# Graph attention, layer 1: masks by casting and transposing DMAs, bias additions by accumulating DMAs, values scaled from PSUM

## The chip, the cores and the metric

The kernel runs on one core of one Trainium2 chip. The metric is the device time of an execution in microseconds (us). Engines are named as in the profile: PE (TensorE; PEld its weight loads), DVE (VectorE), ACT (ScalarE), POOL (GpSimd), SP (SyncE, which issues DMAs). Each engine works through its own instructions in a fixed order, and waits at an instruction until what it needs has been signalled.

## The reference

Two layers, each a graph step and a feed-forward step with residuals, over 32 graphs ("batches") of 512 nodes with 256 features; `adj` (32 x 512 x 512, int32) holds 0 or 1, with ones at about 1 place in 32. Layer 0 (a graph convolution and a tropical feed-forward) is untouched by the change. Layer 1, cut to what matters:

```python
def _L1_gnn_ref(nodes_embed, node_adj, W, a_src, a_dst, bias, ln_gamma, ln_beta):   # H = 4 heads, HO = 64
    h = jnp.einsum('bnd,hde->bhne', nodes_embed, W)
    e_src = jnp.einsum('bhne,hte->bhtn', h, a_src)
    e_dst = jnp.einsum('bhne,hte->bhtn', h, a_dst)
    for t in range(n_types):
        mask = (node_adj == t + 1).astype(h.dtype)[:, None]
        weight = weight + mask * (e_src[:, :, t, :, None] + e_dst[:, :, t, None, :])
    weight = jax.nn.leaky_relu(weight, negative_slope=0.01)
    weight = jnp.where(node_adj[:, None] == 0, NEG, weight)
    attention = jax.nn.softmax(weight, axis=-1)
    dst = jnp.einsum('bhij,bhje->bhie', attention, h) + bias[None, :, None, :]
    out = jax.nn.relu(dst) + h
    mu = out.mean(axis=-1, keepdims=True)
    var = out.var(axis=-1, keepdims=True)
    out = (out - mu) / jnp.sqrt(var + EPS) * ln_gamma[None, :, None, :] + ln_beta[None, :, None, :]
    ...

def _L1_ffn_ref(x, W_fx, b_fx, W_x, b_x, W_slice, b_slice, temperature, ..., out_w, out_b):
    ...
    sw = jax.nn.softmax((xm @ W_slice.T + b_slice) / temp, axis=-1)      # nodes to 64 slices, 8 heads
    st = jnp.einsum('bhnc,bhng->bhgc', fx, sw) / (snorm + 1e-05)[..., None]
    ot = _hydra(st, ...)                                                # two-way scan over the slices
    out = jnp.einsum('bhgc,bhng->bhnc', ot, sw).transpose(0, 2, 1, 3).reshape(B, N, D_INNER)
    return out @ out_w.T + out_b

x = x + _L1_gnn_ref(_layernorm(x, axis=-1), adj, ...)
x = x + _L1_ffn_ref(_layernorm(x, axis=-1), ...)
```

## The kernel before

The fast path of layer 1 is `layer1_plain`. It works through the 32 batches in 16 groups of two. Two streams of work are woven together. `attentions()` is a generator that does the graph attention of one batch after the other (`prepare`, `attention`, `norm`), and runs up to a few batches ahead. `mixer(g)` does the feed-forward of group g: `slices` for each of the two batches, `tokens`, `scan`, then `unslice`. The main loop gives the attention stream a credit of `PACE` for each step of the mixer; `PACE` follows from `TURNS` and `STEPS`, the numbers of steps that a batch takes in `attention` and in `prepare`. So the order of the instructions on every engine is set by where the generators yield, and the program's order is kept.

`prepare(b)` gathers the 512 rows of x by four indirect DMAs of POOL (L1154), waits three steps, normalizes x (statistics L1126 on DVE, a power on POOL in L31, the scaling on ACT in L1133), adds the layernorm's beta to x on POOL (L1167, it belongs to the sum that comes later), turns the normalized rows by PE (L1142), and computes h and the two attention terms by PE. For each of four tiles of 128 nodes ACT takes from PSUM three exponentials (`mine`, a column of `hv`, `other`) and a copy of h (`ht`, L1186). Then POOL adds the attention's bias to `ht` and writes `hv` (L1189), and DVE scales `hv` by the exponential (L1202). `mine` goes through a PE transpose and a DRAM row (`ownd`) to four tiles `own`, one for each head, spread over all partitions; SP issues these DMAs.

The mask of a batch is made by `masks(b)`, woven into the first steps of `prepare`: SP loads four int32 tiles of adj; ACT makes a bf16 copy of each and sums it (L1093), and squares it and sums that (L1094), which serves a test of the input; PE turns the copies (L1084) and DVE writes them as uint8 into `mask` (L1085).

`attention(b)` has eight turns. In each of them DVE makes two weights (L1213): the larger of `own` and `other`, times the mask.

```python
nc.vector.scalar_tensor_tensor(e, own[h], other[:, j, h : h + 1], mask[:, j, :], ALU.max, ALU.mult)
```

PE multiplies them with `hv` into `avp` (values, L1249) and `adp` (denominators, L1254); ACT copies these, PE turns them back, and DVE multiplies by the reciprocal of the denominators into `av`. Since the weights of a node add up to one after that, a bias added to the values before is a bias added to the result. `norm(b, av)` does the relu, the sum with h, the layernorm and the sum into x, in three steps which are taken between the turns of the next batch's attention: all turns but `i == 2`, ending at the first `i > 2`. In it, DVE computes sums, POOL a power for the variance (`mu`, L1300), and DVE multiplies by it (L1303).

`slices(b)` normalizes x again, adds the output's bias `outb` to x on POOL (L1328), and computes the slice weights `sw`: PE (`lgp`), ACT (exponential, L1336), DVE (L1337, a sum L1340, a product L1342), then PE (`yTp`, L1347). `unslice` multiplies back (L1567), DVE adds to x (L1569), SP stores.

At the end, `over` and `flags` say whether the input kept within what the fast path takes for granted (adj of 0 and 1, each node with an edge, terms of moderate size); if not, a general path runs afterwards. With this input it doesn't run.

Buffers: two each of `mask`, `hv`, `ht`; five of x; one of `av`; four PSUM banks of the kind "any".

## Time and profile before

| what | value |
|---|---|
| median of 3 runs | 4460.33 us (4456.45 to 4473.15) |
| the profiled execution's own time | 4459.08 us |
| its span in the trace | 4456.4 us |
| mean granted TensorE clock | 0.948 |
| busy, PE / DVE / ACT / POOL | 3922.0 / 3347.2 / 2291.6 / 1718.8 us |
| `att` L1213, 512 times on DVE | 392.9 us |
| L1189, L1167, L1328, 32 times each on POOL | 80.2, 77.6, 75.8 us |
| L1085, 128 times on DVE | 85.9 us |

Busy times are sums over the span; the sum over engines is more than the span, since they work beside each other. "Idle before" in a row of groups is the time in which the engine stood still just ahead of such instructions, and the name behind it is what ended that. The chain of waits follows the work that ended last back to the beginning, and so shows which time could shorten the whole. Layer 0 takes the span's first 2380 us or so, layer 1 the rest.

### The profile page before, as it was taken

The page shows a single profiled execution, that of the slowest core. Times are in us where ns is not written, and L with a number is a line of the kernel's source. Part 1 is how long each engine was busy: PE and PEld are TensorE (multiplying, and loading weights), DVE is VectorE, ACT ScalarE, POOL GpSimd, SP SyncE. Part 2 cuts the span into 40 slices and gives each one's busy share as a digit, 9 for nine tenths or more (in the row PEclk, how much of TensorE's full clock was granted, in tenths as well). Part 3 has the DMA queues.
Part 4 walks back from the last instruction along what each step waited for, and adds up shares of the span by engine and source line. Part 5 has one row for each costly group of instructions (what it writes and reads, how often), then busy time and mean ns, then how long its engine had stood idle before and what let it go on. Part 6 is the DMA issues. An engine that isn't in the chain of part 4 may idle for free.

```text
span 4456.4 us, 57911 instructions
## 1 busy us (share of the span) xinstructions
PE 3922.0 (88%) x20311; PEld 2470.6 (55%) x20311; DVE 3347.2 (75%) x7008; ACT 2291.6 (51%) x4756; POOL 1718.8 (39%) x2036
## 2 busy tenths in 40 slices
PE   5568898899988999888997899999999999999987
PEld 4454565566656656545554455555555555555555
DVE  6668887897788987877766777767677877778763
ACT  3345565566564665556654544544545444454433
POOL 2357644664446644454314232332222232332220
PEclk8679999999999999989998999999999999999998
DMA  5546543664436543564422111111111111111100
GB/s 133 160 144 223 190 130 122 210 200 139 156 117 213 187 147 129 162 201 167 138 81 67 36 53 57 56 48 58 51 43 42 53 55 55 58 48 58 41 15 16
DMA packets 235107, 474.21 MB, mean 106 GB/s; under 512 B 38299, under 2 KB 114075, under 8 KB 234804
## 3 DMA queue, kind: packets, MB, share of 16 engines
q0 software_dynamic: 98688, 315.94, 22.2%
q1 hardware_dynamic: 136116, 154.46, 11.0%
q8 instruction: 162, 2.65, 0.2%
q14 instruction: 141, 1.16, 0.1%
HBM read 413.16 MB, written 57.16 MB: 106 GB/s over the span
## 4 chain that ended last, share of the span: by engine, by line
DVE 34%; PE 32%; DMA 11%; issue 9%; POOL 9%; ACT 5%; SPq 0%; POOLq 0%; DVEq 0%; ACTq 0%
DVE att L1213 5%; DVE acc L637 4%; PE clsp L623 3%; PE avp L1249 3%; PE po L652 3%; PE gatep L623 3%; DMA rows<-table,xs 2%; PE yTp L1347 2%; DVE sw L1337 2%; DVE sw L1342 2%; DVE best L598 2%; DMA rows<-table,tops 2%; DVE sst L1340 2%; DMA best<-table,xs 2%; PE xp L1400 1%
## 5 line engine op out<-in xcount | busy, mean ns | idle before, releaser
L623 PE MATMUL clsp<-xnT,wc 128*128 128x512 f32 x1024 | 520.8, 627 | 49.7 <-ACT cls L625 37.6
L623 PE MATMUL gatep<-xnT,wg 128*128 128x512 f32 x1024 | 499.8, 607 | 10.5 <-ACT gate L625 7.7
L652 PE MATMUL po<-wd,acc 128*128 128x256 f32 x2048 | 455.4, 381 | 6.1 <-DVE acc L641 3.8
L1213 DVE SCALAR_TENSOR_TENSOR att<-own,other,mask 128x512 f32<-128x512 f32 x512 | 392.9, 796 | 79.0 <-DMA own<-ownd 79.0
L652 PEld LDWEIGHTS po<-wd,acc 128*128 128x128 f32 x2048 | 388.3, 191 | 72.1 <-issue 9.2
L598 DVE SCALAR_TENSOR_TENSOR best<-rows,xs,best 128x1024 f32<-128x1024 f32 x212 | 274.4, 1295 | 121.9 <-ACT best L592 76.4
L637 DVE SCALAR_TENSOR_TENSOR acc<-past,fld,acc 128x512 f32<-128x512 f32 x448 | 345.7, 775 | 24.9 <-ACT past L636 16.9
L632 ACT ACTIVATE acc<-tz,fld 128x512 f32<-128x512 f32 x256 | 198.8, 777 | 269.3 <-PE tz L630 240.1
L623 PEld LDWEIGHTS gatep<-xnT,wg 128*128 128x128 f32 x1024 | 196.0, 196 | 252.3 <-issue 197.9
L636 ACT ACTIVATE past<-tz,fld 128x512 f32<-128x512 f32 x448 | 291.4, 693 | 68.1 <-DVE acc L637 66.6
L1347 PE MATMUL yTp<-sw,x 128*128 128x512 f32 x512 | 264.6, 655 | 64.3 <-DVE sw L1342 59.6
L595 POOL DMA_INDIRECT rows<-table,xs x212 | 249.5, 1177 | 171.6 <-DVE best L598 119.0
L1249 PE MATMUL avp<-att,hv 128*32 128x512 f32 x2048 | 298.9, 607 | 5.6 <-DVE att L1213 5.6
L623 PEld LDWEIGHTS clsp<-xnT,wc 128*128 128x128 f32 x1024 | 181.5, 198 | 188.1 <-issue 111.8
L434 PE MATMUL pm<-h,adj 128*128 128x258 f32 (+1 forms) x1024 | 181.2, 324 | 99.9 <-DVE keep L427 33.7
L1300 POOL TENSOR_TENSOR mu<-mu,eps 128x16 f32<-128x16 f32 x32 | 111.6, 3487 | 391.1 <-DVE mu L1299 391.0
L1335 PE MATMUL lgp<-wsl,x4T 128*128 128x512 f32 x512 | 242.8, 613 | 15.7 <-ACT sw L1336 6.8
L1154 POOL DMA_INDIRECT x<-x2s,ranks x128 | 135.9, 1062 | 298.1 <-DVE att L1213 148.1
L625 ACT ACTIVATE gate<-gatep,fld 128x512 f32<-128x512 f32 x256 | 175.5, 685 | 142.6 <-PE gatep L623 123.8
L553 POOL DMA_INDIRECT xs<-rows_of,order x128 | 156.1, 1219 | 221.5 <-DVE acc L637 100.8
L1567 PE MATMUL outp<-v,swT 128*128 128x256 f32 x1024 | 227.6, 381 | 0.0
L625 ACT ACTIVATE cls<-clsp,fld 128x512 f32<-128x512 f32 x256 | 176.1, 688 | 93.9 <-PE clsp L623 55.6
(599 smaller groups left out, 8978.1 us busy)
## 6 DMA issues: line engine op xcount, KB each, us to landing
adj<-in_adj POOLq DMA_DIRECT2D x128, 256.0 KB
ai<-in_adj SPq DMA_DIRECT2D x128, 256.0 KB
own<-ownd SPq DMA_DIRECT2D x128, 256.0 KB
rows_of<-keep SPq DMA_DIRECT2D x32, 550.0 KB
x<-in_x SPq DMA_DIRECT2D x32, 512.0 KB
x2s<-xs SPq DMA_DIRECT2D x32, 512.0 KB
out<-x SPq DMA_DIRECT2D x32, 512.0 KB
rows<-table,xs POOLq DMA_INDIRECT x212
```

Of the source, the lines that this page charges most:

```text
L595: nc.gpsimd.indirect_dma_start(out=row, out_offset=None, in_=table, in_offset=bass.IndirectOffsetOnAxis(ap=idxs[:, k : k + 1].bitcast(U32) ...
L598: nc.vector.scalar_tensor_tensor(m, row, vals[:, k : k + 1], m, ALU.add, ALU.max)
L623: nc.tensor.matmul(pf, wf[:, c, f * P : (f + 1) * P], xnT[:, c, :], start=c == 0, stop=c == DC - 1)
L625: nc.scalar.activation(o, pf, fn, bias=fld[:, f, bf : bf + 1], scale=1.0 if fn == AF.Gelu else 0.5)
L636: nc.scalar.activation(r, z, AF.Relu, bias=fld[:, f, AT + b : AT + b + 1])
L637: nc.vector.scalar_tensor_tensor(y, r, fld[:, f, CH + b : CH + b + 1], y, ALU.mult, ALU.add)
L652: nc.tensor.matmul(po[:, i, :], acc[f][:, t * P : (t + 1) * P], wd[:, f, :], start=f == 0, stop=f == FC - 1)
L1213: nc.vector.scalar_tensor_tensor(e, own[h], other[:, j, h : h + 1], mask[:, j, :], ALU.max, ALU.mult)
L1249: nc.tensor.matmul(pv[p][k * HW : (k + 1) * HW, :], hv[:, j, h, e : e + HW], weighed[b, h, j], **ends)
L1335: nc.tensor.matmul(pf, xnT[:, c, t * P : (t + 1) * P], wsl[:, c, :], start=c == 0, stop=c == DC - 1)
L1347: nc.tensor.matmul(py, xn[:, t, c * P : (c + 1) * P], sw[:, t, :], start=t == 0, stop=t == NT - 1)
L1567: nc.tensor.matmul(po[:, :D], swT[:, k, t * P : (t + 1) * P], v[:, k, :], start=k == 0, stop=k == KC - 1)
```

## The change

The masks are made by DMAs: two batches ahead POOL issues a DMA that casts adj (int32) to bf16 into a DRAM tile `short`, and SP issues a transposing DMA from it into `mask`, now bf16. In place of the sums for the test, ACT takes a Square of mask - 0.5 over the whole mask with its sum (each element gives 0.25 if it is 0 or 1), and DVE marks denominators that are not above 0.

The three additions of POOL (beta, the attention's bias, outb) become accumulating DMAs which POOL issues, from rows in a small DRAM table `added`. The attention's bias is added to `av` after the attention, ahead of `norm`, whose three steps start one turn later. `hv` is now written by DVE directly from PSUM, right after the exponential that it is scaled by, for each tile of 128 nodes.

`STEPS` goes from 15 to 11, and with it `PACE` from 0.887 to 0.765. The constants `identb`, `abias`, `beta` and `outb` are gone. In the changed kernel lines have other numbers; those spoken of are L1282 (norm's first instruction on DVE, which takes the relu and adds h), L1292 (the power, L1300 before) and L1295 (the product with it, L1303 before).

```diff
@@ -887,7 +887,7 @@
     HE = HO + 1
     AP = AH // 2
     TURNS = AP * NT + 6
-    STEPS = 15
+    STEPS = 11
     WANTED = 68
     AHEAD = 3
     ATT = 2 * (AHEAD + 2) + AP + 1
@@ -915,8 +915,6 @@
 
         ones = ctile("ones", [P, P])
         nc.gpsimd.memset(ones, 1.0)
-        identb = cst.tile([P, P], BF16, tag="identb", name="identb")
-        nc.vector.tensor_copy(identb, ident)
 
         wa = ctile("wa", [P, DC, AH * HO + 2 * AH])
         for c in range(DC):
@@ -940,14 +938,24 @@
                                  start=c == 0, stop=c == DC - 1)
             nc.vector.tensor_scalar(over[:, : 2 * AH], pn[:, : 2 * AH], SMALL, None, ALU.is_gt)
         yield
-        edges = ctile("edges", [P, 2, B * NT])
-        abias = const("abias", [P, AH * HO], w["gnn_bias"].rearrange("h e -> (h e)").partition_broadcast(P))
+        edges = ctile("edges", [P, B + B * NT])
+        centre = ctile("centre", [P, 1])
+        nc.gpsimd.memset(centre, -0.5)
+        added = dr.tile([3, NT, D], F32, tag="added", name="added", bufs=1)
+        for i, row in enumerate((w["gnn_bias"].rearrange("h e -> (h e)"), w["ln_beta"].rearrange("h e -> (h e)"),
+                                 w["out_b"])):
+            nc.sync.dma_start(added[i], row.partition_broadcast(NT))
+        added = added.rearrange("i t d -> i (t d)")
+        ABIAS, BETA, OUTB = range(3)
+
+        def add_rows(dst, i):
+
+            nc.gpsimd.dma_start(dst, added[i].partition_broadcast(P), accum_op=ALU.add)
+
         gamma = const("gamma", [P, AH * HO], w["ln_gamma"].rearrange("h e -> (h e)").partition_broadcast(P))
-        beta = const("beta", [P, AH * HO], w["ln_beta"].rearrange("h e -> (h e)").partition_broadcast(P))
         bfx = const("bfx", [P, KC, 1], w["b_fx"].rearrange("(k p o) -> p k o", p=P, o=1))
         bfx_eps = ctile("bfx_eps", [P, KC])
         nc.vector.tensor_scalar_mul(bfx_eps, bfx[:, :, 0], -1e-5)
-        outb = const("outb", [P, D], w["out_b"].partition_broadcast(P))
         conv_w = const("conv_w", [P, KC, KW], w["hy_conv_w"][:DI].rearrange("(c p) k -> p c k", p=P))
         conv_b = const("conv_b", [P, KC], w["hy_conv_b"][:DI].rearrange("(c p) -> p c", p=P))
         bc_w = const("bc_w", [S, 2, KW], w["hy_conv_w"][DI:].rearrange("(c p) k -> p c k", p=S))
@@ -1068,44 +1076,24 @@
             nc.scalar.activation(ebsl, ebsl, AF.Exp)
 
         se = ctx.enter_context(tc.tile_pool(name="e1", bufs=2, side="right", reuse_waits="tile"))
-        masked = {}
-
-        def masks(b, bank="any"):
-
-            a, raw = [], []
-
-            def load(t):
-                raw.append(se.tile([P, N], I32, tag="ai", name=f"ai{b}_{t}", bufs=2))
-                nc.sync.dma_start(raw[t], adj[b, t * P : (t + 1) * P, :])
-
-            def turn(t):
-                pt = ps.tile([P, NT, P], BF16, tag=bank, name=f"maskp{b}_{t}")
-                for j in range(NT):
-                    nc.tensor.transpose(pt[:, j, :], a[t][:, j * P : (j + 1) * P], identb)
-                nc.vector.tensor_copy(mask[:, :, t * P : (t + 1) * P], pt)
-
-            load(0)
-            load(1)
-            yield
-            for t in range(NT):
-                n = b * NT + t
-                a.append(se.tile([P, N], BF16, tag="a", name=f"a{b}_{t}", bufs=3))
-                nc.scalar.activation(a[t], raw[t], AF.Identity, accum_out=edges[:, 0, n : n + 1])
-                nc.scalar.activation(raw[t], raw[t], AF.Square, accum_out=edges[:, 1, n : n + 1])
-                if t + 2 < NT:
-                    load(t + 2)
-                if t == 1:
-                    mask = se.tile([P, NT, N], mybir.dt.uint8, tag="mask", name=f"mask{b}")
-                    yield
-                if t > 1:
-                    turn(t - 2)
-                    yield
-            for t in range(NT - 2, NT):
-                turn(t)
-                yield
-            masked[b] = mask
-
-        yield from masks(0, "mm")
+        short, masked = {}, {}
+
+        def shorten(b):
+
+            if b < B:
+                short[b] = dr.tile([N, N], BF16, tag="short", name=f"short{b}", bufs=3)
+                tc.keep_in_program_order(nc.gpsimd.dma_start(short[b], adj[b], max_dma_last_dim=8192))
+
+        def turn(b):
+
+            if b < B:
+                masked[b] = se.tile([P, NT, N], BF16, tag="mask", name=f"mask{b}")
+                nc.sync.dma_start_transpose(masked[b], short.pop(b))
+
+        for b in range(2):
+            shorten(b)
+            yield
+        turn(0)
         yield True
         ps = ctx.enter_context(tc.tile_pool(name="p1", bufs=4, space=PSUM, reuse_waits="tile"))
         sb = ctx.enter_context(tc.tile_pool(name="s1", bufs=2, reuse_waits="tile"))
@@ -1158,20 +1146,23 @@
 
             hv = sb.tile([P, NT, AH, HE], F32, tag="hv", name=f"hv{b}")
             xn = hv.rearrange("p t h e -> p (t h e)")[:, : NT * D].rearrange("p (t d) -> p t d", t=NT)
-            edged = masks(b) if b not in masked else range(3)
-            for i, _ in enumerate(edged):
-                if i < 3 or b not in masked:
-                    yield
-                if i == 2:
-                    normed(xt, xn, f"c{b}")
-                    nc.gpsimd.tensor_add(xt, xt, beta.unsqueeze(1).to_broadcast([P, NT, D]))
-                    yield
+            if b:
+                turn(b)
+            shorten(b + 2)
+            yield
+            yield
+            yield
+            normed(xt, xn, f"c{b}")
+            add_rows(xt.rearrange("p t d -> p (t d)"), BETA)
+            yield
             mask = masked.pop(b)
             xnT = yield from turned(xn, "x3T", f"x3T{b}")
             yield
 
 
             ht = sb.tile([P, NT, AH * HO], F32, tag="ht", name=f"ht{b}")
+            nc.scalar.activation(ht.rearrange("p t e -> p (t e)").bitcast(BF16), mask.rearrange("p t n -> p (t n)"),
+                                 AF.Square, bias=centre, accum_out=edges[:, b : b + 1])
             other = sb.tile([P, NT, AH], F32, tag="other", name=f"other{b}")
             mine = sb.tile([P, AH, NT], F32, tag="mine", name=f"mine{b}")
             for t in range(NT):
@@ -1180,15 +1171,14 @@
                     nc.tensor.matmul(ph[:, : AH * (HO + 2)], xnT[:, c, t * P : (t + 1) * P], wa[:, c, :],
                                      start=c == 0, stop=c == DC - 1)
                 d = ph[:, AH * HO : AH * HO + AH]
+                nc.scalar.activation(hv[:, t, :, HO], d, AF.Exp)
+                nc.vector.tensor_mul(hv[:, t, :, :HO], ph[:, : AH * HO].rearrange("p (h e) -> p h e", h=AH),
+                                     hv[:, t, :, HO:].to_broadcast([P, AH, HO]))
                 nc.scalar.activation(mine[:, :, t], ph[:, AH * (HO + 1) : AH * (HO + 2)], AF.Exp, scale=1.0 - SLOPE)
-                nc.scalar.activation(hv[:, t, :, HO], d, AF.Exp)
                 nc.scalar.activation(other[:, t, :], d, AF.Exp, scale=SLOPE - 1.0)
                 nc.scalar.copy(ht[:, t, :], ph[:, : AH * HO])
                 yield
 
-            nc.gpsimd.tensor_add(hv[:, :, :, :HO], ht.rearrange("p t (h e) -> p t h e", h=AH),
-                                 abias.rearrange("p (h e) -> p h e", h=AH).unsqueeze(1).to_broadcast([P, NT, AH, HO]))
-            yield
             pt = psum("any", f"minep{b}")
             nc.tensor.transpose(pt[: AH * NT, :P], mine.rearrange("p h t -> p (h t)"), ident)
             row = sb.tile([AH * NT, P], F32, tag="turned", name=f"turned{b}", bufs=1)
@@ -1198,8 +1188,6 @@
             own = [wide("own", f"own{b}_{h}", AH + 1) for h in range(AH)]
             for h in range(AH):
                 nc.sync.dma_start(own[h], own_row[h].partition_broadcast(P))
-            for t in range(NT):
-                nc.vector.tensor_mul(hv[:, t, :, :HO], hv[:, t, :, :HO], hv[:, t, :, HO:].to_broadcast([P, AH, HO]))
             ready[b] = mask, ht, hv, other, own
             yield
 
@@ -1254,10 +1242,10 @@
                         nc.tensor.matmul(pd[h * HW : (h + 1) * HW, :], hv[:, j, h, HO:].to_broadcast([P, HW]),
                                          weighed.pop((b, h, j)), **ends)
                 yield
-                if unfinished and i != 2:
+                if unfinished and i not in (0, 3):
                     next(unfinished[0], None)
                     yield
-                    if i > 2:
+                    if i > 3:
                         unfinished.pop()
             dT = wide("att", f"adT{b}", ATT)
             nc.scalar.copy(dT, pd)
@@ -1266,6 +1254,8 @@
                 nc.scalar.copy(vT[q], pv[q])
             yield
             dt = back(dT, "dp")
+            nc.vector.tensor_scalar(edges[:, B + b * NT : B + (b + 1) * NT],
+                                    dt.rearrange("p (t e) -> p t e", t=NT)[:, :, 0], 0.0, None, ALU.is_le)
             rs = sb.tile([P, NT, AH], F32, tag="rs", name=f"rs{b}")
             nc.vector.tensor_scalar_max(rs, dt.rearrange("p (t h e) -> p t h e", t=NT, h=AH)[:, :, :, 0], 1e-30)
             nc.vector.reciprocal(rs, rs)
@@ -1275,6 +1265,8 @@
                 nc.vector.tensor_mul(av[:, :, heads, :], bt.rearrange("p (t h e) -> p t h e", t=NT, h=2),
                                      rs[:, :, heads].unsqueeze(3).to_broadcast([P, NT, 2, HO]))
                 yield
+
+            add_rows(av.rearrange("p t h e -> p (t h e)"), ABIAS)
             unfinished.append(norm(b, av))
 
         unfinished = []
@@ -1325,7 +1317,7 @@
             normed(xt, xn, f"d{b}")
             yield 5
             xnT = yield from turned(xn, "x4T", f"x4T{b}", 1)
-            nc.gpsimd.tensor_add(xt, xt, outb.unsqueeze(1).to_broadcast([P, NT, D]))
+            add_rows(xt.rearrange("p t d -> p (t d)"), OUTB)
             sw = sb.tile([P, NT, DI], F32, tag="sw", name=f"sw{b}", bufs=1)
             swT = sb.tile([P, KC, N], F32, tag="swT", name=f"swT{b}")
             yield 2
@@ -1598,10 +1590,9 @@
 
 
         flags = over[:, 2 * AH + 3 :]
-        nc.vector.tensor_sub(flags, edges[:, 1, :], edges[:, 0, :])
-        nc.vector.tensor_scalar(flags, flags, 0.0, None, ALU.not_equal)
-        nc.vector.tensor_scalar(edges[:, 0, :], edges[:, 0, :], 0.5, None, ALU.is_lt)
-        nc.vector.tensor_add(flags, flags, edges[:, 0, :])
+        nc.vector.tensor_copy(flags, edges[:, B:])
+        nc.vector.scalar_tensor_tensor(flags[:, :B], edges[:, :B], 0.25 * NT * N, flags[:, :B],
+                                       ALU.not_equal, ALU.add)
 
 
 def layer1(tc, ident, eps, x2, adj, w, out):
```

## The prediction

> **What bounds the kernel now.** I read the page first (shares of engines, chain, costliest groups), then the table of windows, because the change touches only layer 1, the second half of the span.
>
> ```profile
> PE 3922.0 (88%) x20311; PEld 2470.6 (55%) x20311; DVE 3347.2 (75%) x7008; ACT 2291.6 (51%) x4756; POOL 1718.8 (39%) x2036
> DVE 34%; PE 32%; DMA 11%; issue 9%; POOL 9%; ACT 5%; SPq 0%; POOLq 0%; DVEq 0%; ACTq 0%
> ```
>
> No engine is busy all the time, and the chain passes between DVE and PE. Layer 1 runs from about 2400 us to the end in 16 groups of two batches, 125.3 us apart (the starts of the groups' first outp matmuls, 2574.6 to 4332.0 us). Its windows read PE, PEld, DVE, ACT, POOL busy, clock, DMA share, GB/s:
>
> ```profile
> 3020.00:3522.00 502.00, 467.07 (x3064) 279.67 (x3064) 366.00 (x786) 245.68 (x632) 146.47 (x112) 0.97 0.16 51
> ```
>
> PE shows 93%, but a busy PE is not PE at its peak. From the spacing of the matmuls I put the real streaming at 107 us per group: the gap of 18 us per group is what layer 1 could give, 18 x 15.5 groups (the last is shorter) = 280 us. DVE has 92 us of work per group (922.8 us in the 1250 us from 3020 to 4270), so it isn't full either. A group has two halves: some 55 us (the scan) in which PE streams, and some 70 us in which DVE works through att, sw, sst and norm and the others wait for it.
>
> The groups the change touches (operation, count | busy, mean ns | idle before, releaser):
>
> ```profile
> L1189 POOL TENSOR_TENSOR hv<-ht,abias 128x1024 f32<-128x1024 f32 x32 | 80.2, 2506 | 81.2 <-ACT ht L1186 81.2
> L1328 POOL TENSOR_TENSOR x<-x,outb 128x1024 f32<-128x1024 f32 x32 | 75.8, 2370 | 126.8 <-ACT x L1133 125.9 <-PE x4T3p L1142 0.8
> L1202 DVE TENSOR_TENSOR hv<-hv 128x256 f32<-128x256 f32 x128 | 46.6, 420 | 177.5 <-POOL hv L1189 177.5
> L1085 DVE CAST mask<-maskp 128x512 uint8<-128x512 bf16 x128 | 85.9, 676 | 1.2 <-PE maskp L1084 0.8
> L1084 PE MATMUL maskp<-identb,a 128*128 128x128 bf16 x512 | 45.5, 221 | 11.5 <-ACT sw L1336 7.0 <-DVE mask L1085 3.3 <-ACT a L1093 1.2
> L1303 DVE TENSOR_TENSOR av<-av,mu 128x1024 f32<-128x1024 f32 x32 | 39.1, 1221 | 26.0 <-POOL mu L1300 26.0
> ```
>
> The waits of DVE from 2600 to 4270 us (total, times, longest):
>
> ```profile
> DVE hv L1202 <- POOL hv L1189: 154.5, 27, 8.9
> DVE att L1213 <- DMA own<-ownd: 72.8, 13, 7.3
> ...
> DVE av L1303 <- POOL mu L1300: 19.8, 13, 2.1
> ```
>
> The first is the largest stall of DVE: 5.7 us each, once per batch. The POOL addition of the attention bias comes just before DVE's scaling of hv, and DVE is in order. The POOL and the DVE timeline of one group:
>
> ```profile
> 3377.52 2.38 POOL L1328 TENSOR_TENSOR x<-x,outb 128x1024 f32<-128x1024 f32 x1 [0.26 <-ACT x L1133]
> 3382.70 2.35 POOL L1189 TENSOR_TENSOR hv<-ht,abias 128x1024 f32<-128x1024 f32 x1 [2.80 <-ACT ht L1186]
> 3385.08 1.10 DVE L1202 TENSOR_TENSOR hv<-hv 128x256 f32<-128x256 f32 x3 [7.62 <-POOL hv L1189]
> ```
>
> **A rule, and its row.** The Trainium skill, "SBUF — State Buffer", section "SBUF: two separate sides", says that VectorE and GpSimd share a pair of ports as an exclusive lock: a VectorE operation with two SBUF inputs is held back for the whole of a GpSimd instruction that reads SBUF. The trace agrees:
>
> ```profile
> 3356.49 3.26 DVE L1337 TENSOR_TENSOR sw<-sw,ebsl 128x512 f32<-128x512 f32 x1
> 3356.82 2.37 POOL L1167 TENSOR_TENSOR x<-x,beta 128x1024 f32<-128x1024 f32 x1
> ```
>
> That product takes 0.69 us where POOL is quiet; it ends as the addition does. Over layer 1, 35 DVE instructions are stretched by the three additions, 68.5 us in all (59.0 of it by L1167), 4.4 us per group. With the additions made by DMA engines this goes. For an accumulating DMA the trace has no row. "DMA: Bandwidth & Descriptors", section "Anatomy of one DMA — SWDGE (gpsimd) path", fits such a transfer as 2.0 us plus bytes/436e3, so an estimate of 3.2 us for 512 KB. The nearest row, the 512 KB gathers in 4 KB rows (rows<-table), land 5.4 to 7.2 us after their issue. I go by the row, at its low end, since a plain pattern needs no indices: L = 5.5 us. The bounds are 3.5 us (the 128 KB gather of x lands in 3.3 to 3.9) and 10 us (the same traffic doubled, if the sum's old value is read through the same engines).
>
> **What goes.** Per group of two batches: six POOL additions (14.6 us of POOL), 8 mask casts of DVE (8 x 0.68 = 5.4 us), 32 PE transposes (about 1.8 us at their pitch of 56 ns), on ACT the two passes over four adj tiles with their accumulator reads (13.3 us), eight adj loads on SP. What of it lies on the path is read from the chain of waits, 3020 to 4270 us: hv L1189 23.5 us, x L1328 21.4, mask L1085 21.3, maskp L1084 10.4, together 76.6 us in 9.8 groups = 7.8 per group. Of the 4.4 us of stretching I count 3, since most of it falls in the half that DVE sets. Sum 10.8 us per group, x 15.5 = 167 us. The rest was hidden beside PE, and costs nothing to lose.
>
> **What moves without cost.** DVE's scaling is as before four products of 256 columns per batch (0.42 us), now from PSUM and right after ACT's exponential: same work, no POOL between. mask as bf16 in att: still two f32-rate inputs and one output; the f32 product of three operands in L637 takes 775 ns against att's 796, so the type decides nothing (bounds 0 to 0.05 us x 32 per group). The flags from dp: 0.15 us per batch, nothing. Casting DMAs (a 1 MB read, 0.5 MB written, two batches ahead, some 60 us early) and the transposing DMA: 0.16 of the DMA engines is in use, so even a doubling leaves them free; their cover is those 60 us. Without it att would wait for the whole transfer. The transposing DMA has no row. It stands on SP's queue ahead of ownd and own of the batch before, by 25 to 30 us; from nothing up to that it costs nothing; beyond it, all own would be late. POOL's issues: one cast and three accumulations per batch at 0.6 to 1.0 us (L392's DMAs: 575 ns, gathers: 1062) in place of 7.2 us of additions.
>
> **What is added as waits, per group.**
>
> 1. The bias is now added to av by a DMA that POOL issues after DVE's last product with rs, and norm's first DVE instruction (L1282 of the changed kernel) waits for it, with PE's norm products of the slices and the next att queued behind on DVE. The change starts norm one turn of attention later, and the order of DVE shows what covers the landing: seven att of 0.7 us in the even batch, 5 us; in the odd one an att and two additions of x, about 3 us. The stall is (L - 5) + (L - 3) = 2L - 8: 3.0 us at L = 5.5; zero at 4; 12 at 10.
> 2. The power on POOL (3.5 us, L1292 after) now stands behind four gathers (5.2 us) and a rsqrt, while DVE's product with mu (L1295) comes right behind, where sw and sst work stood between. The stall in order is 5 to 6 us in one batch of two; it was 1.6 (26.0 us over 16 groups, row L1303). On the path, with PE still holding work of the slices: 1.8, bounds 0 to 4.
> 3. The wait for own. Its chain is mine, transpose, ownd (3.4 us), own (3.3 us); part of it lay under the wait for hv that goes. So of the 11.4 us saved in stalls some reappears as `att <- own`; at most 4 us per group, taken 2.
> 4. ACT: mine now waits for DVE's product that reads the same PSUM, and a Square over the mask (2.1 us, twice L1296's 1.05) stands ahead of the exponentials. ACT is half idle; 1 us, bounds 0 to 2.
>
> Returned: 3.0 + 1.8 + 2.0 + 1.0 = 7.8 us per group. Net gain 10.8 - 7.8 = 3.0, x 15.5 = 46 us, and some 3 us at the start of layer 1, where batch 0's mask no longer passes ACT, PE and DVE. From the profiled execution's own time of 4459.1 us (span 4456.4 and 2.7 around it): 4410 us. The median of the three runs is 1.2 us above that; I leave it.
>
> The pace (STEPS 15 to 11) lowers the credit of attention per step of the mixer from 0.89 to 0.77, following the removed steps; the order shows it as evenly woven as before, so nothing.
>
> **Rivals.**
> A, the waits do not come back (accumulations land within cover, own is under att): the 10.8 us stay, and reach 167 us: 4292 us. For it: 18 us per group of PE idle. Against it: L would have to be under 4, and att <- own already costs 72.8 us with the old cover.
> B, no change: the hv wait is replaced one for one by waits for own and mu (items 2 to 4 at their upper bounds, 10 us, with L at 4): 4455 us. For it: att <- own is already the second wait of DVE, and its two transfers in a row haven't changed.
> C, slower: L is long. With items 2 to 4 at 4.8 us, break-even is 2L - 8 = 6.0, so L = 7 us. At L = 10, 12 + 4.8 - 10.8 = 6 us per group lost: 4552 us. For it: the accumulation must read what it adds to; the row itself reaches 7.2; and x's next gather is behind norm's end. Against: DMA engines mostly idle.
> D, the edit does not do what it says, since ACT would still hold the masks: excluded by the order, where the four loads and eight passes are gone.
>
> **Numbers.** Forecast case (gain of 22 to 110 us) 0.37; A 0.13; B 0.15; C with its milder forms 0.35. A measurement of this kernel tells 0.5% (22 us) from no change. That makes faster 0.50, same 0.15, slower 0.35. The range goes from 4300 (just short of A) to 4535 (most of C); the likeliest case's own is 4350 to 4438.
>
> **What would show it.** Right: `DVE hv <- POOL hv` gone; a wait of DVE's av (L1282) for av's DMA of about 1.5 us a batch, a wait for mu of up to 5 us in one batch of two; `att <- own` above 72.8 us; sw products at 0.69 us throughout; period near 122 us. Wrong: av waiting over 3.5 us a batch on average (C), or masks landing so late that att waits for them; a period of 115 us or less (A).

## The result and the profile after

The changed kernel takes 4508.61 us (median of 4 runs, 4494.63 to 4515.02) against 4458.39 us before (4 runs): ratio 1.0105, 95% interval 1.0075 to 1.0134. So it is slower by 50 us, where the forecast was 4410 us, a gain of 49. The profiled execution took 4515.0 us, with a span of 4513.3.

The first rows of the page: engines, then the chain by engine.

```profile
PE 3933.4 (87%) x19799; PEld 2468.0 (55%) x19799; DVE 3204.0 (71%) x6909; ACT 2198.0 (49%) x4305; POOL 1570.2 (35%) x2069
PE 32%; DVE 31%; DMA 15%; issue 9%; POOL 8%; ACT 4%; SPq 1%; DVEq 0%; POOLq 0%; ACTq 0%
```

The work went as planned: DVE has 143 us less to do, ACT 94, POOL 149. The chain has not become shorter: DMA takes 655 us of it where it took 480, and in layer 1 the new parts are the landing of the bias (151 us) and the store of x (83 us). A window of layer 1 (columns as in the prediction) and some groups of instructions:

```profile
3020.00:3522.00 502.00, 460.79 (x2924) 275.03 (x2922) 319.60 (x738) 221.99 (x516) 108.30 (x119) 0.97 0.33 75
```

```profile
L1282 DVE SCALAR_TENSOR_TENSOR av<-av,ht 128x1024 f32<-128x1024 f32 x32 | 39.2, 1225 | 54.8 <-DMA av<-added 54.8
L1295 DVE TENSOR_TENSOR av<-av,mu 128x1024 f32<-128x1024 f32 x32 | 39.2, 1225 | 162.1 <-POOL mu L1292 162.1
```

The share of the DMA engines doubled from 0.16 to 0.33. In the rows, the last column is what matters: the product with mu now has 162.1 us of idle time before it (26.0 before), the start of norm 54.8. The waits of DVE from 2600 to 4270 us (total, times, longest) say the same:

```profile
DVE av L1295 <- POOL mu L1292: 149.1, 26, 9.9
DVE rms L1538 <- PE msp L1535: 92.9, 13, 7.9
DVE sw L1329 <- ACT sw L1328: 88.2, 13, 6.8
...
DVE av L1282 <- DMA av<-added: 43.2, 26, 4.5
...
DVE att L1201 <- DMA own<-ownd: 3.7, 7, 0.9
```

Two rows beside the one for mu are large as well: DVE waits 92.9 us for PE's `msp`, 11.2 before, and 88.2 us for ACT's exponentials `sw`, which are not in the list of before. The experiments come back to them.

Groups are now 128.6 us apart (125.5 before; means over the same 14 groups). How a stall comes about is read from the chain of one group (start, duration, what):

```profile
3365.69 0.70 DVE av L1265
3366.39 0.29 issue
3366.68 5.34 DMA av<-added
...
3372.14 1.23 DVE av L1282
3373.37 0.33 DVE x L1561
...
3375.16 0.32 DVE x L1561
3375.48 0.03 DVE mu L1285
3375.51 7.61 DMA out<-x
...
3388.70 0.61 POOL short L1085
3389.30 2.97 POOL mu L1292
3392.28 0.02 issue
3392.30 0.04 DVE av L1295
```

The bias lands 5.3 us after its issue. Norm's first instruction waits for it on DVE, and the last two additions to x wait behind that one. The store of x waits for those additions, and takes 7.6 us. POOL's gathers of the next x need the buffer that the store empties; they, the cast, and then the power of norm follow in POOL's queue. The two timelines beside this, DVE and POOL:

```profile
3381.28 0.17 DVE L1291 TENSOR_SCALAR mu<-mu 128x16 f32<-128x16 f32 x1
3381.36 1.41 DVE L1201 SCALAR_TENSOR_TENSOR att<-own,other,mask 128x512 f32<-128x512 f32 x2
3392.30 1.22 DVE L1295 TENSOR_TENSOR av<-av,mu 128x1024 f32<-128x1024 f32 x1 [9.53 <-POOL mu L1292]
```

```profile
3383.88 1.06 POOL L1142 DMA_INDIRECT x<-x2s,ranks  x1 [3.84 <-DMA out<-x]
```

The power's input is ready at 3381.45 (the end of L1291), and the power starts at 3389.30. DVE stands for 9.5 us, and behind it stand all the slice weights of the batch, so PE too. It is so in one batch of each group: in all 13 groups between 2600 and 4270 us the power starts 5.3 to 8.2 us after its input is ready, 90.6 us in all, and DVE then stands for 7.0 to 9.9 us. In the other batch it starts at once, and DVE waits 2.8 us.

One correction to what is told of the kernel above: the order on an engine is not always the program's order. Building the program reorders instructions: here it put these four gathers ahead of a power that the program issues earlier, as the run with the power first will show.

### The profile page after: what moved, and what is told of

Its sections match the earlier page's. It is cut to its first block, busy times and chain, and to the rows that moved or that the text cites. A ratio compares the mean times of both kernels' runs of the same rounds, so it can differ in the third digit from the quotient of the medians.

```text
span 4513.3 us, 56135 instructions
## 1 busy us (share of the span) xinstructions
PE 3933.4 (87%) x19799; PEld 2468.0 (55%) x19799; DVE 3204.0 (71%) x6909; ACT 2198.0 (49%) x4305; POOL 1570.2 (35%) x2069
## 3 DMA queue, kind: packets, MB, share of 16 engines
q1 hardware_dynamic: 183836, 137.30, 10.4%
## 4 chain that ended last, share of the span: by engine, by line
PE 32%; DVE 31%; DMA 15%; issue 9%; POOL 8%; ACT 4%; SPq 1%; DVEq 0%; POOLq 0%; ACTq 0%
DVE acc L637 4%; PE clsp L623 4%; PE po L652 4%; DMA av<-added 3%; PE yTp L1339 3%; PE gatep L623 3%; PE outp L1559 3%; POOL mu L1292 2%; DMA rows<-table,xs 2%; DMA out<-x 2%; DMA rows<-table,tops 2%; DVE best L598 2%; PE oTp L1527 2%; DVE att L1201 2%; PE avp L1237 2%
## 5 line engine op out<-in xcount | busy, mean ns | idle before, releaser
L1201 DVE SCALAR_TENSOR_TENSOR att<-own,other,mask 128x512 f32<-128x512 f32 x512 | 358.3, 737 | 12.8 <-DMA own<-ownd 12.8
L1237 PE MATMUL avp<-att,hv 128*32 128x512 f32 x2048 | 333.0, 601 | 7.2 <-DVE att L1201 7.2
L1339 PEld LDWEIGHTS yTp<-sw,x 128*128 128x128 f32 x512 | 104.9, 214 | 227.5 <-DVE sw L1334 126.2
L434 PEld LDWEIGHTS pm<-h,adj 128*128 128x128 f32 x1024 | 152.8, 215 | 129.2 <-issue 73.4
```

Of the source, the lines that this page charges most:

```text
L434: nc.tensor.matmul(pm[:, : c1 - c0], a[:, i, t * P : (t + 1) * P], h[:, i, c0:c1], start=i + c0 == 0, stop=i + 1 == NT and c0 > 0)
L1237: nc.tensor.matmul(pv[p][k * HW : (k + 1) * HW, :], hv[:, j, h, e : e + HW], weighed[b, h, j], **ends)
L1339: nc.tensor.matmul(py, xn[:, t, c * P : (c + 1) * P], sw[:, t, :], start=t == 0, stop=t == NT - 1)
```

## The experiments

The theory from the two traces, Q: the loss lies in the queues, where the bias accumulated last makes norm wait and norm's power stands behind gathers that wait for a store. The first rival, D: the DMA engines, which have twice the load, make transfers late. Others (L, P, F, T, V) are put in the expectations as they came up. There are 16 runs. Where an expectation speaks of the fifth experiment, it means the changed kernel with the power first; the tenth is that one without the bias, the eleventh the masks and two additions with the power first. Ratios are to the kernel before (4460 to 4462 us in these sets), with a 95% interval. The edits are shown shortened: `...` and plain words stand for code that is left out.

**The parts alone.** First, only the masks by DMAs:

```diff
 (the changed kernel)
-add_rows(xt..., BETA) / add_rows(xt..., OUTB) / add_rows(av..., ABIAS)
+nc.gpsimd.tensor_add(xt, xt, beta...) / (xt, xt, outb...) / (hv, ht, abias...), hv scaled as before
-if unfinished and i not in (0, 3):      # norm's turns as before
+if unfinished and i != 2:
-STEPS = 11
+STEPS = 12
```

> Edit: the changed kernel with only the masks by DMAs kept; the three bias additions and the scaling of hv are as in the kernel before (STEPS 12). Theory Q (the loss is in the order on POOL and DVE: the bias accumulated last makes norm wait, and its power then stands behind gathers that wait for a store): the masks alone are not the cause, so faster than before by 20 to 60 us (5.4 us of DVE casts, 1.8 us of PE and 2.5 us of chain per group go), about 4420. Theory D (the DMA engines: the casting and transposing DMAs load them twice as much, and the store, own and the gathers land later): slower than before or equal, 4460 to 4500, with the store's landing at 7 us instead of 4.4.

4492.1 us, 1.0073 (1.0054 to 1.0092). DVE waits 90.6 us for mu where it waited 19.8; so the masks lose, against theory Q as it was put. Theory D had the time right, but its sign in the trace is mixed: in the chain stores of x land in 2.9 to 4.8 us in some places and in 6.4 to 7.5 in others. The masks with the power first, further down, tell more.

Only beta and outb:

```diff
 (the kernel before)
-nc.gpsimd.tensor_add(xt, xt, beta.unsqueeze(1).to_broadcast([P, NT, D]))
+add_rows(xt.rearrange("p t d -> p (t d)"), BETA)
-nc.gpsimd.tensor_add(xt, xt, outb.unsqueeze(1).to_broadcast([P, NT, D]))
+add_rows(xt.rearrange("p t d -> p (t d)"), OUTB)
```

> Edit: the kernel before with only beta and outb added to x by accumulating DMAs. Theory Q: faster by 30 to 60 us, about 4415 (4.4 us per group of stretched DVE instructions and 2.1 us of chain go; nothing near waits for the landings). Theory D: no gain, 4450 to 4480, since 1 MB more per batch passes the same engines.

4367.9 us, 0.9795 (0.9775 to 0.9814), a gain of 92 us, more than theory Q had. The row of the slice products, which POOL's additions had stretched (834 ns mean before), shows the larger part of why:

```profile
L1346 DVE TENSOR_TENSOR sw<-sw,ebsl 128x512 f32<-128x512 f32 x128 | 86.4, 679 | 11.0 <-ACT sw L1345 11.0
```

Over layer 1, DVE instructions stretched by a POOL addition fall from 68.5 us to 2.1. This fits the exclusive lock told of in the Trainium skill, "SBUF — State Buffer", section "SBUF: two separate sides", which the two additions no longer take. The outb addition itself also stood on the chain (21.4 us in 1250); how the 92 us divide between the two is not shown. The order on DVE hardly changed: it differs at some 20 of 7008 instructions.

Only the bias last:

```diff
 (the kernel before)
-nc.gpsimd.tensor_add(hv[:, :, :, :HO], ht..., abias...)   # and the scaling of hv in SBUF
+nc.vector.tensor_mul(hv[:, t, :, :HO], ph..., hv[:, t, :, HO:]...)
+add_rows(av.rearrange("p t h e -> p (t h e)"), ABIAS)
-if unfinished and i != 2:
+if unfinished and i not in (0, 3):
-STEPS = 15
+STEPS = 14
```

> Edit: the kernel before with only the attention's bias accumulated last into av, hv scaled from PSUM, and norm one turn later (STEPS 14). Theory Q: this is the part that loses: slower by 50 to 110 us, 4510 to 4570, DVE's wait for mu at 8 us or more in one batch of two, its wait for the hv addition gone. Theory D: within 20 us of before, 4440 to 4480.

4571.4 us, 1.0235 (1.0209 to 1.0261), 111 us lost: this is the part. But DVE waits only 14.7 us for mu here (19.8 before), so the power is not what it pays for; its waits for `msp` (85.7 us) and `sw` (84.6 us) are as large as in the changed kernel. The three parts come to -92 + 32 + 111 = +51 us, and the whole change to +50. That is luck: the runs below show that the price of a part depends on what stands beside it.

**The wait and the power.** The changed kernel without the accumulation into av:

```diff
-add_rows(av.rearrange("p t h e -> p (t h e)"), ABIAS)
```

> Edit: the changed kernel without the accumulation of the attention's bias into av (the bias, zero in this input, isn't added at all). Theory L (the landing of 5.2 us ahead of norm is itself the loss, with what stands behind it on DVE): returns 60 to 100 us of the changed kernel's time, about 4430. Theory Q with the power behind the gathers as the larger part: returns 20 to 50 us, about 4475, and DVE's wait for mu stays at 8 us or more per group. Theory D: returns about 10 us.

4445.1 us, 0.9968 (0.9957 to 0.9979): 63 us return, as theory L had it; yet the wait for mu fell too, from 149.1 to 57.0 us, and no power is late any more, against what theory Q expected. So a run has to part the two. The next one queues the gathers of x behind the power (`issue_after` holds what it encloses behind an instruction), where the program has issued that power already:

```diff
+powered[b] = nc.gpsimd.tensor_tensor(mu[:, 1, :], ..., ALU.pow).ins
+with tc.issue_after(powered.pop(b - 3)):     # in prepare, around the gathers
     for t in range(NT):
         nc.gpsimd.indirect_dma_start(...)
```

> Edit: in the changed kernel, POOL's four gathers of a batch are queued behind the power of norm three batches before, which stood behind them; nothing else. Theory Q (the power's place on POOL is what costs beside the landing): DVE's wait for mu falls from 11.5 to 3 us per group or less, and the time by 40 to 90 us, to about 4445. Theory L (the landing of the bias alone matters, and DVE would then wait for something else): less than 20 us, about 4495.

4434.2 us, 0.9949 (0.9933 to 0.9966): 74 us return, and the changed kernel is faster than before. The edit is a clean one: past the start of layer 1 the order on POOL differs only in the place of 13 powers, and that on DVE at some 40 of 6909 instructions in all. No power is late. Its waits:

```profile
DVE av L1298 <- POOL mu L1295: 65.0, 27, 2.8
...
DVE av L1285 <- DMA av<-added: 42.1, 27, 3.5
```

The wait for the bias is as long as it was (42.1 against 43.2 us); the wait for mu fell by more than half. With both edits:

```diff
 (the kernel of the run before)
-add_rows(av.rearrange("p t h e -> p (t h e)"), ABIAS)
```

> Edit: the changed kernel with the power first and without the accumulation of the attention's bias (which isn't added at all). If the landing costs through the power alone (each removes the same stall), about 4430, as each of the two alone. If the two costs lie one after the other on the path, their gains add: 4509 - 63 - 74 = 4371.

4434.2 us, 0.9932 (0.9916 to 0.9948), the same median as with the bias. The four kernels make a square: 4509 us, 4445 without the bias, 4434 with the power first, 4434 with both. So in the order of the change, the landing costs through the power: it delays x, its store and the gathers, and the power behind them. Once the power is out of that queue, DVE's 3.3 us per group for the landing cost nothing that can be measured, because another wait takes their place: without the bias DVE waits 76.5 us for the gathers of x where it waited 35.9.

**The masks with the power first.**

```diff
 (the kernel with only the masks by DMAs)
+with tc.issue_after(powered.pop(b - 3)):     # around the gathers
```

> Edit: the kernel with only the masks by DMAs (4492 us), and the gathers queued behind the power as in the fifth experiment. Theory Q (the masks lose for the same reason: power and store wait on POOL, here 90.6 us of DVE's waits for mu between 2600 and 4270 us): 4430 to 4455, so the masks themselves gain little or nothing against before. Rival F (the casts and passes that went were filler under other waits): 4475 to 4495.

4466.5 us, 1.0012 (1.0002 to 1.0023). 26 us come back (in the masks alone 9 of 26 powers were late, by 38.4 us together; here none is), and the masks are then even. That lies between the ranges of theory Q and of rival F. As F has it, 5.4 us of casts per group bought nothing; that they were filler under other waits is argued, not shown.

**Pace and DMA load.** The credit as before, in the changed kernel and in the kernel with only the masks:

```diff
-PACE = 1.04 * GB * (TURNS + STEPS) / WANTED
+PACE = 1.04 * GB * (TURNS + 15) / WANTED
```

> Edit: the changed kernel with the credit of the attention stream as before (PACE 0.887 in place of 0.765). Theory P (the lower pace puts the attention's later parts among the slices, where the waits are): returns 30 to 70 us, about 4460. Theory Q: the same waits are met in another place, 4490 to 4530.

> Edit: the kernel with only the masks by DMAs (4492 us) with the credit as in the kernel before (0.887 in place of 0.796). Theory P: the masks themselves gain, and the pace lost it: 4410 to 4440. Rival F (the casts and passes that went were filler under waits for POOL and PE, which stay; the new order lets DVE reach those waits sooner): within 20 us of 4492.

4766.6 us (1.0693, 1.0675 to 1.0711) and 4708.2 us (1.0566, 1.0545 to 1.0586). Theory P has the wrong sign: the lower pace belongs to the fewer steps, and without it over 200 us are lost, which none of the theories had. Paces in between were not tried, so a better one may exist.

The cast moved away from the store:

```diff
-shorten(b + 2)      # behind the gathers
+shorten(b + 2)      # at the end of prepare
```

> Edit: the changed kernel with the casting DMA of adj issued at the end of a batch's preparation instead of right behind its gathers. Theory D (the cast's 1.5 MB stands in the way of the store of x, which lands in 7.6 us instead of about 4): the store's landing returns to 4 to 5 us, and 20 to 45 us come back, about 4475. Theory Q: the store is 7 us for other reasons, and less than 10 us come back.

4529.7 us, 1.0153 (1.0134 to 1.0173), some 20 us slower than the changed kernel. POOL's wait for stores of x fell from 56.9 to 23.0 us, as theory D says, and the twelve stores whose landing the trace has took 2.9 to 3.8 us; but own is now late:

```profile
DVE att L1201 <- DMA own<-ownd: 55.2, 23, 5.5
```

That row had 3.7 us. SP's issues show how. The 8 KB store `ownd` must land before own can be issued; in the first of these two batches it was issued 3.4 us behind a cast, in the second no cast was on its way:

```profile
3414.49 0.33 SPq L1186 DMA_DIRECT2D ownd<-turned  x1
3419.41 1.80 SPq L1189 DMA_DIRECT2D own<-ownd  x4
...
3479.64 0.32 SPq L1186 DMA_DIRECT2D ownd<-turned  x1
3481.00 1.75 SPq L1189 DMA_DIRECT2D own<-ownd  x4
```

That is 4.9 us against 1.4; from 2900 to 3690 us it is 4.0 to 5.6 in the seven batches with a cast just ahead, and 1.3 to 2.5 in the others. Moved, the cast only finds another victim. So theory D is right about the transfers, and wrong about what moving the cast returns.

**Which part of "bias last" is dear.** Masks and the two additions by DMAs, the attention's bias as before, the power first:

```diff
 (the changed kernel, power first)
-add_rows(av..., ABIAS), hv scaled from PSUM, norm one turn later, STEPS = 11
+bias added to hv by POOL, hv scaled in SBUF, norm's turns as before, STEPS = 12
```

> Edit: the masks by DMAs, beta and outb by accumulating DMAs, the attention's bias and the scaling of hv as in the kernel before, the power first. If the parts add (92 us gained by the additions, the masks about even once the power is first): 4350 to 4380, and this is as good as the two additions alone (4368) or better. If the DMA engines are the limit (masks and accumulations in each other's way): above 4400.

4355.1 us, 0.9761 (0.9747 to 0.9775): the best of all, 105 us below the kernel before; the intervals of this and of the two additions alone just touch at 0.9775, and the two additions with the power first but without the masks were not run. Against the 4434 us of the whole change with the power first, the bias part still costs 79 us, even where no bias is added. Norm another turn later:

```diff
 (the changed kernel, power first)
-if unfinished and i not in (0, 3):
+if unfinished and i not in (0, 1, 4):
```

> Edit: the changed kernel with the power first and norm another turn of attention later (steps at turns 2, 3 and 5), so that more att covers the bias's landing. Theory L (the rest of the loss is DVE's wait for the landing, 42 us between 2600 and 4270): 4390 to 4410. Rival: norm's end, which slices and the store wait for, moves by the same amount, 4430 to 4470.

4585.1 us, 1.0266 (1.0247 to 1.0286). DVE's wait for the bias has shrunk to 0.8 us, and the time is 151 us longer than with the power first alone. This is worse than the rival had it, and points at the turn. Four runs test it. Undone where no bias is added, then made alone:

```diff
 (no bias, power first)
-if unfinished and i not in (0, 3):
+if unfinished and i != 2:
```

> Edit: the kernel of the tenth experiment (the changed kernel, power first, the attention's bias not added at all) with norm's steps at the turns of before. Theory T (norm one turn later costs the 79 us): about 4360. Theory V (the scaling of hv from PSUM costs them): about 4430.

```diff
 (masks and two additions, power first)
-if unfinished and i != 2:
+if unfinished and i not in (0, 3):
```

> Edit: the kernel of the eleventh experiment (masks and two additions by DMAs, power first, bias and hv as before) with norm's steps one turn later, as in the change, and nothing else. Theory T: about 4430. Theory V: about 4355.

4373.8 us (0.9802, 0.9790 to 0.9815) and 4581.2 us (1.0281, 1.0265 to 1.0297). Theory T holds in both: the turn is worth 60 us in the first pair and 226 us in the second. The waits of DVE with norm a turn later, and in the second fence with the old turn (both without the bias, power first):

```profile
DVE sw L1331 <- ACT sw L1330: 94.9, 14, 6.8
DVE rms L1540 <- PE msp L1537: 86.4, 13, 7.9
...
DVE att L1204 <- DMA own<-ownd: 3.5, 6, 1.1
```

```profile
DVE att L1204 <- DMA own<-ownd: 68.6, 14, 5.9
DVE rms L1540 <- PE msp L1537: 55.7, 13, 4.3
...
DVE sw L1331 <- ACT sw L1330: 35.7, 28, 3.3
```

The large waits for `sw` and `msp` thus come with the turn, and so does the small one for own. The two kernels at the old turn, 4374 and 4355, differ by 19 us; besides the scaling from PSUM they differ in the bias addition on POOL and in STEPS (11 and 12), so theory V isn't measured by itself. With the turn alone DVE's list is headed by

```profile
DVE stc L1115 <- DMA x<-x2s,ranks: 124.3, 73, 5.0
DVE rn L1352 <- ACT swT L1351: 102.1, 15, 9.3
DVE att L1208 <- DMA own<-ownd: 99.2, 31, 8.4
```

instead of norm: the gathers of x and own now come late. Why it is 226 us in one place and 60 in the other isn't settled; the turn moves many instructions at once.

The whole change with the old turn, with the power first and without:

```diff
-if unfinished and i not in (0, 3):
+if unfinished and i != 2:
```

> Edit: the changed kernel, whole, with the power first and norm's steps at the turns of before, so that the bias's landing has one turn less of cover. Theory T: below the 4434 of the fifth experiment, 4380 to 4410, with a longer wait of DVE for av. Theory V: 4450 to 4500, since the landing is uncovered and nothing is gained.

> Edit: the changed kernel, whole, with norm's steps at the turns of before and nothing else (its power again behind the gathers). Theory T: 4440 to 4480, a gain on the changed kernel's 4509. Theory V: 4520 to 4570.

4551.5 us (1.0201, 1.0188 to 1.0214) and 4466.6 us (1.0008, 0.9993 to 1.0023). The first contradicts theory T's number: with less cover, the wait for the bias is 77.8 us, and holding the gathers behind a power that itself waits for the bias makes them late (78.7 us of DVE's waits for them). Theory V's 4450 to 4500 missed it as well. The second gains 42 us on the change, as theory T had it, with 86.9 us of waits for the bias; there no power is late even without the pin, so it was the later turn that brought the power behind the gathers. The turn and the landing are traded against each other: at the old turn DVE stands for the bias, at the later one it stands elsewhere.

## Why the prediction was wrong

With the runs the loss can be written as a row of steps, each with what the prediction had for it (its us per group times 15.5):

| step | forecast, us | measured, us | from, to |
|---|---|---|---|
| masks and two additions by DMAs (power first) | -130 | -105 | 4460, 4355 |
| hv scaled from PSUM, bias left out (with own and ACT) | +9 | +19 | 4355, 4374 |
| norm a turn later | 0 | +60 | 4374, 4434 |
| the bias accumulated | +46 | 0 | 4434, 4434 |
| the power behind the gathers | +28 | +74 | 4434, 4509 |
| sum | -46 | +48 | |

This is one way through the runs, and the steps are not independent: with the bias accumulated and the power first, the later turn does not cost but gain (4552 to 4434).

- **Step 2 failed, "On the path, with PE still holding work of the slices: 1.8".** In order the stall was put at 5 to 6 us in one batch of two. It is 8.7 us in that batch and 2.8 in the other (149.1 us in 13.0 groups, 11.5 per group), and by the run with the power first 74 / 15.5 = 4.8 us per group of the path, above the upper bound of 4. Only the gathers' own 5.2 us and a small power (rsqrt) had been counted as standing ahead. The first gather itself waits for the store of x, the store for additions behind the landing on DVE, and the cast's issue comes on top. Nor did PE hold work: its waits for the last slice product are 82.8 us where they were 56.8 (44.5 with the power first), since DVE reaches those products only after the product with mu. The prediction had named this queue without following what the first in it waits for, and none of its signs of being wrong was a long wait for mu.
- **The turn was costed at nothing.** "The change starts norm one turn of attention later, and the order of DVE shows what covers the landing" took the turn for cover alone. It costs 60 us (4374 to 4434), 3.9 us per group, where no bias has to be covered, and with the old turn the whole change loses 42 us less.
- **The landing's length was right, its price was not.** L was put at 5.5 us, and most landings in the chain are 4.8 to 5.5; the stall of 3.0 us per group is 43.2 / 13.0 = 3.3. As a term of its own, beside the power, it costs nothing. The row of the 512 KB gathers was the better guide than the 3.2 us worked out from the Trainium skill, "DMA: Bandwidth & Descriptors", section "Anatomy of one DMA — SWDGE (gpsimd) path". Rival C, slower through a long L, has the sign and not the mechanism; that the time lies within the range given, 4300 to 4535, is owed to C's share of it.
- **Masks.** 3.2 of the 10.8 us per group (21.3 + 10.4 us of chain over 9.8 groups) were put down as gain, 50 us. The masks alone lost 32 us and were even with the power first: the casts lay on the chain, and taking them away still shortened nothing. That the mask's type decides nothing held: an att takes 744 ns with uint8 and 743 with bf16 (medians).
- **Two additions.** 3 us of stretching and 2.2 of outb per group, 80 us, measured 92.
- **own.** A loss of 2.0 us per group was taken; its wait shrank from 72.8 to 3.7 us, since own has mostly landed when DVE comes to it. That is the turn again: with the old turn the wait is 62.2 to 68.6 us, about as before, so the removed wait for hv did not turn into it either.
- **ACT and the scaling from PSUM.** 1.0 us per group forecast. It was not measured alone; the 19 us of the table's second row, 1.2 per group, hold it together with the rest of that step.
- **DMA load.** "Even a doubling leaves them free" was the wrong question. The share did double, to 0.33, and the engines were far from full; but single transfers became longer: a store of x that lands in 2.93 us in the chain before takes 6.0 to 8.0 in the chain after, and the run with the cast moved shows the cast's part in it.
- **Slips in the working.** The starts of the groups give 125.5 us, not 125.3, and so 10.0 groups in 1250 us, not 9.8. Rival B's sum comes to 4447 us, not 4455. The stretched product starts 0.33 us before the addition and ends 0.56 us after it, not with it. None of them changes the forecast by more than 3 us.

## What to carry to other kernels

Before a wait is added or a DMA put on an in-order queue, follow the queue through: what the instruction ahead waits for, and what that waits for in turn, over the engines; here it was four links from a bias that nobody needed soon to a small power that everybody needed. Removing busy time from an engine can gain nothing, as with the masks, but taking two additions off POOL, which had stretched 68 us of DVE's instructions, gained 92 us. Test the parts of a change one by one: two of these additions gave most of the 105 us of the best kernel, and the third, with the turn that came with it, cost 111 us alone. And test them together too: the later turn cost 60 us in one place and 226 in another, and gained 117 in a third.

## What the runs showed of the hardware

TensorE's granted clock can fall after short gaps, but need not. The matmuls of oTp (32 of them, of 128 columns) take 3.84 us in 14 of the 16 groups of the kernel before, and in the first 14 groups of the changed kernel 3.84 us in seven and about 5.4 in seven. Windows (columns as above; the first row of each pair is the stretch ahead of oTp, the second oTp): two groups of the changed kernel, and in the second fence one of the kernel before.

```profile
3470.00:3477.60 7.60, 4.96 (x47) 3.69 (x45) 4.42 (x9) 5.01 (x22) 0.91 (x1) 1.00 0.38 71
3477.60:3483.10 5.50, 5.47 (x36) 5.35 (x38) 0.00 (x0) 0.02 (x1) 0.00 (x0) 0.69 0.54 189
3600.30:3607.90 7.60, 4.95 (x47) 3.69 (x45) 4.41 (x9) 5.01 (x22) 0.90 (x1) 1.00 0.41 71
3607.90:3611.80 3.90, 3.88 (x36) 3.76 (x37) 0.00 (x0) 0.00 (x1) 0.00 (x0) 1.00 0.22 44
```

```profile
3440.00:3446.60 6.60, 5.76 (x53) 3.96 (x51) 1.38 (x2) 5.04 (x23) 2.78 (x2) 1.00 0.12 40
3446.60:3450.50 3.90, 3.85 (x34) 3.73 (x36) 1.43 (x4) 0.62 (x2) 1.95 (x1) 1.00 0.22 71
```

With PE 65% busy ahead of it, oTp ran at a granted clock of 0.69 in one group and at 1.00 in another; with 87%, at 1.00. No gap in the two stretches of the changed kernel was longer than 1.3 us by PE's timeline. The Trainium skill, "TensorE: Matmul & The Clock Gate", section "What's actually happening", tells of an idle window of about 3.4 us after which the clock falls; here shorter gaps, 2.6 us out of 7.6 together, went ahead of it. But in six of the other groups the same gaps went ahead of the full clock, so they do not decide it alone; what does is open, and no run changed them by themselves. As an estimate from these times, the seven slower groups cost 7 x 1.6 = 11 us.
